# Splitting the first context load, its product and their order at the start of a cross-attention kernel

## The chip, the cores and the metric

The kernel runs on one core of a Trainium2 chip. The metric is the device time of one execution in microseconds (us); the median of three runs of the kernel before is 794.72 us (794.46 to 795.08). A core has five engines that work side by side and wait for one another through semaphores: TensorE (PE in the profile, with its weight loads as PEld), VectorE (DVE), ScalarE (ACT), GpSimd (POOL) and SyncE (SP), which here issues nearly all transfers (DMAs). Each engine takes its instructions strictly in the order of the program.

## What is computed

The inputs are `x` (8 x 128 x 512) and a context (8 x 128 x 512), all float32. The reference, cut to what matters:

```python
x = x + xattn(layernorm(x), ctx, ctx, mask, Wq, Wk, Wv, Wo)   # 32 query heads, 8 key/value heads of 128
x = x + ffn(layernorm(x), nf4(w1), nf4(w2), nf4(w3))          # weights quantized to NF4 and back, H = 1376
# in xattn:  k = rope(ctx @ Wk);  v = ctx @ Wv;  q = rope(layernorm(x) @ Wq)
#            softmax over 30*tanh(q.k*scale/30), masked, times v, times Wo
```

Only `k = rope(ctx @ Wk)` is touched by the change, and of it only the first of the 16 key products.

## The kernel before, in words

**Precision by halves.** A float32 operand is split in two fp32r tiles, a high part and a low part. `split` (lines 154 to 156) does it: ScalarE casts the source into the high part (line 155), then VectorE or GpSimd subtracts that from the source into the low part (line 156). `product` (lines 165 to 171) makes a float32 product of three matmuls for each slice of the contraction: high weights with low data (line 169), high with high (line 170), low with high (line 171). The contraction is 512 long, in KT = 4 slices of 128, so one product is 12 matmuls.

**Stages.** The kernel first computes all keys and values and stores them to DRAM, then runs 64 attention steps, then the feed-forward part. The change lies in the first microseconds of the first stage. This stage works through a list written out by hand, `tiles` (line 571): `("k", kv, half)` is the key product of head `kv` over one half of the context's 1024 rows (512 of them), `("v", j, b)` a value product, `("q", 0, g)` a first query product. It begins k(0,0), k(1,0), k(2,0), k(0,1), k(1,1), k(2,1), then values and keys take turns.

**Key product.** `k_proj` (line 511) writes pk(kv, half), one PSUM bank of 128 x 512, from the split weights `wkt[kv]` and the split, transposed context `cT`. Banks with the tag "q" are two in number, so k(2,0) has to wait until k(0,0)'s bank has been read. The reading is `rope` (line 454): two ScalarE copies of half the partitions each, from PSUM into `rs_k` with the halves exchanged (lines 461, 462), a VectorE product of PSUM with the cosine table into `rc_k` (line 463), a GpSimd product of `rs_k` with the sine table (line 464), and an addition into `kr` (line 465; on VectorE for heads 0 to 2). `rs_k` and `rc_k` have two buffers each. The loop at line 628 sets the order: at tile n it emits the rope of tile n-1 without its addition, then the product n, then the addition of tile n-2, then what `advance(n)` gives, then the extras of `plan[n]`.

**Loads.** `loads` (line 585) lists what is loaded and the tile from which on its split may be emitted. `advance(n)` (line 592) issues loads ahead of time, as long as `early` (the eight accumulator tiles, not yet needed, used as landing buffers) has buffers or fewer than four loads wait for their split, and it emits the splits that are due, in list order. All loads go through SP's queue. Before, the order at the start is:

```python
loads = [(-1, "k", 0, 0)] + [(-1, "c", 0, k) for k in range(KT)]
loads += [(-1, "t", 0, 0), (-1, "k", 1, 0), (0, "k", 2, 0), (0, "c", 1, 0), (0, "c", 1, 1), (1, "c", 1, 2), (1, "c", 1, 3)]
```

Here ("k", kv) is the key weights of head kv, 256 KB; ("c", half, k) is slice k of the context's half `half`, 128 x 512 floats, 256 KB in rows of 2 KB; "t" is the table of cosines and sines `tab`, 2 x 128 x 128 floats, 128 KB in rows of 512 bytes. In the text they are called wk0, c00 to c03, the table, wk1, wk2, c10 to c13. The low part of wk0 and of the context is made on VectorE, that of wk1 and wk2 on GpSimd. The splits of wk2, c10 and c11 are emitted at tile 0, so ahead of the rope of k(0,0); those of c12 and c13 at tile 1, behind it.

Of the kernel before, what the change touches and what calls it, by code (L numbers as in the profile page):

```python
# [20 lines left out]
P = 128  # L21
# [4 lines left out]
KT = D // P  # L26
# [36 lines left out]
def block_kernel(ctx: ExitStack, tc: tile.TileContext, x, ctxt, mask, wq, wk, wv, wo, w1, w2, w3, w12t, w3_t,  # L63
                 rope_tab, nf_bias, out):
    nc = tc.nc
    V, S, Q, E = nc.vector, nc.scalar, nc.gpsimd, nc.tensor
# [9 lines left out]
    def bank(tag, name):  # L76
        shape = [P, 1024 if tag == "pv" else 512]
        return ps.tile(shape, F32, tag=tag, name=name, bufs=2 if tag == "q" else 1)[:, :512]
# [75 lines left out]
    def split(hi, lo, src, engine):  # L154
        S.copy(hi, src)
        engine.tensor_tensor(lo, src, hi, ALU.subtract)  # L156
# [5 lines left out]
            E.transpose(pt[:, k * P:(k + 1) * P], src[:, k * P:(k + 1) * P], ident)  # L162
        return lambda: split(hi, lo, pt.rearrange("p (k t) -> p k t", k=KT), V)

    def product(out, pairs, start=True, stop=True):

        n = len(pairs)
        for i, ((ah, al), (bh, bl)) in enumerate(pairs):
            E.matmul(out, ah, bl, start=start and i == 0, stop=False)  # L169
            E.matmul(out, ah, bh, start=False, stop=False)  # L170
            E.matmul(out, al, bh, start=False, stop=stop and i == n - 1)  # L171


    def scales(a, r, w):
# [251 lines left out]
    with ExitStack() as c1:  # L426
# [9 lines left out]
        early = list(acc)  # L436

        def stage(src, shape, name):
            if early:
                raw = early.pop(0)  # L440
            else:
                raw = raw_pool[-1].tile([P, 512], F32, tag="raw", name=f"raw_{name}", bufs=3 if len(raw_pool) > 1 else 4)
            if len(shape) == 3:
                raw = raw.rearrange("p (k n) -> p k n", k=shape[1])
            nc.sync.dma_start(raw, src)
            return raw
# [7 lines left out]
        def rope(dst, src, cos, sgn, name, engine=None):  # L454

            hd = HD // 2
            every = lambda ap: ap.unsqueeze(1).to_broadcast([P, 4, T])
            src4 = src.rearrange("p (b t) -> p b t", t=T)
            c = tp.tile([P, 4, T], F32, tag="t1", name=f"rc_{name}")
            s = tp.tile([P, 4, T], F32, tag="t2", name=f"rs_{name}")  # L460
            S.copy(s[:hd], src4[hd:])
            S.copy(s[hd:], src4[:hd])  # L462
            V.tensor_tensor(c, src4, every(cos), ALU.mult)  # L463
            Q.tensor_tensor(s, s, every(sgn), ALU.mult)  # L464
            return lambda: (engine or Q).tensor_tensor(dst, c, s, ALU.add)  # L465
# [6 lines left out]
        def q_proj(u, g):  # L472
            kv, half = divmod(u, 2)
            if g == 0:
                qr[u] = a1.tile([P, 4, G, T], F32, tag="qr", name=f"qr_{u}", bufs=2)
            pq = bank("q", f"pq_{u}_{g}")
            w, t = wqt[kv, g], xT[half]
            product(pq, [((w[:, 0, k], w[:, 1, k]), (t[:, 0, k], t[:, 1, k])) for k in range(KT)])
            return lambda: rope(qr[u][:, :, g, :], pq, cosq, sgnq, f"q{u}_{g}", V if u < 2 else None)


        with ExitStack() as c3:
# [4 lines left out]
            cT = [kv1.tile([P, KT, B * T], F32R, name=f"cT_{i}", bufs=1) for i in range(2)]  # L487
# [3 lines left out]
            def load_c(half, k):  # L491
                cols = slice(half * 512, half * 512 + 512)
                raw = stage(ctxt[k * P:(k + 1) * P, cols], [P, 512], f"c_{half}_{k}")
                return lambda: split(cT[0][:, k, cols], cT[1][:, k, cols], raw, V)

            def load_v(j, k):
                raw = stage(wv[k * P:(k + 1) * P, j * 512:(j + 1) * 512], [P, 512], f"wv_{j}_{k}")
                if (j, k // 2) not in wvt:
                    wvt[j, k // 2] = kv1.tile([P, 2, 2, 512], F32R, tag="wv", name=f"wv_{j}_{k}", bufs=3)
                t = wvt[j, k // 2]  # L500
                return lambda: split(t[:, 0, k % 2], t[:, 1, k % 2], raw, (V, Q)[j])
# [9 lines left out]
            def k_proj(kv, half):  # L511
                cols = slice(half * 512, half * 512 + 512)
                pk = bank("q", f"pk_{kv}_{half}")
                w = wkt[kv]
                product(pk, [((w[:, 0, k], w[:, 1, k]), (cT[0][:, k, cols], cT[1][:, k, cols])) for k in range(KT)])

                def later():
                    kr = kv1.tile([P, 512], F32, tag="kr", name=f"kr_{kv}_{half}")
                    add = rope(kr.rearrange("p (b t) -> p b t", t=T), pk, tab[:, 0], tab[:, 1], f"k{kv}_{half}",
                               V if kv < 3 else Q)  # L520

                    def last():
                        add()
                        nc.sync.dma_start(kr_d[kv, half], kr)
                    return last
                return later

            def v_proj(j, b):
                own = slice(b * T, b * T + T)
                pv = bank(("pv", "wo")[b % 2], f"pvp_{j}_{b}")  # L530
                product(pv, [((cT[0][:, k, own], cT[1][:, k, own]),
                              (wvt[j, k // 2][:, 0, k % 2], wvt[j, k // 2][:, 1, k % 2])) for k in range(KT)])

                def later():
                    v = vs[:, b % 4]
                    S.copy(v, pv.rearrange("p (a d) -> p a d", a=4))
                    return lambda: nc.sync.dma_start(
                        v_d[4 * j:4 * j + 4, :, b, :].rearrange("a p d -> p a d"), v)
                return later
# [26 lines left out]
            def normal(b):  # L566
# [8 lines left out]
                     ("v", 1, 1), ("k", 7, 1)] + [("v", 1, b) for b in range(2, B)] + [("q", 0, g) for g in range(G)]  # L575
            make = {"k": k_proj, "v": v_proj, "q": q_proj}
            plan = [[] for _ in range(len(tiles) + 1)]


            def load_tab(*_):  # L580
                nc.sync.dma_start(tab, rope_tab.rearrange("c d t -> d c t"))
                return lambda: None

            load = {"t": load_tab, "k": load_k, "c": load_c, "v": load_v, "q": load_first_q}
            loads = [(-1, "k", 0, 0)] + [(-1, "c", 0, k) for k in range(KT)]
            loads += [(-1, "t", 0, 0), (-1, "k", 1, 0), (0, "k", 2, 0), (0, "c", 1, 0), (0, "c", 1, 1), (1, "c", 1, 2), (1, "c", 1, 3)]
            loads += [(2, "v", 0, 0), (2, "v", 0, 1), (3, "v", 0, 2), (3, "v", 0, 3), (5, "k", 3, 0), (9, "k", 4, 0)]
            loads += [(12, "k", 5, 0), (15, "k", 6, 0), (17, "v", 1, 0), (18, "v", 1, 1), (19, "k", 7, 0)]
            loads += [(20, "v", 1, 2), (21, "v", 1, 3)] + [(24 + 2 * g, "q", g, 0) for g in range(G)]
# [78 lines left out]
        def where(i):  # L668
            u, bb = divmod(i, 4)
            return u, u // 2, (u % 2) * 4 + bb, bb  # L670
# [88 lines left out]
        for i in range(N):  # L759
            u, kv, b, bb = where(i)  # L760
# [101 lines left out]
    pairs = {}  # L862
    for b, i in down:
# [5 lines left out]
        for h in range(4 * i, min(NHT, 4 * i + 4)):  # L869
            m = min(P, H - h * P)  # L870
            t, s = w3t[h].rearrange("p i k c -> p i (k c)"), hs[b, i]
# [7 lines left out]
        elif i == 2:  # L879
            o = f1.tile([P, D], F32, tag="o", name=f"o_{b}", bufs=4)  # L880
            parts = 2 if b == B - 1 else 1
            for j in range(parts):
                own = slice(j * D // parts, (j + 1) * D // parts)
# [38 lines left out]
```

## Time and profile before

| what | value |
|---|---|
| median of 3 runs | 794.72 us |
| the profiled execution's own time | 795.47 us |
| its span, first to last instruction | 793.7 us |
| mean granted TensorE clock | 0.998 |
| busy: PE, PEld | 779.9 us (98%), 628.8 us (79%) |
| busy: DVE, ACT, POOL | 633.7 us (80%), 586.3 us (74%), 469.4 us (59%) |
| PE busy, 5 to 10 us | 3.11 of 5.00 us |
| PE busy, 20 to 100 us | 79.55 of 80.00 us |

Busy times are sums over an engine's instructions in one profiled execution; the span is that of the same execution, and 1.77 us of the execution's time lie around the span. A matmul's end is modelled and overlaps the next one, so the pace of matmuls is read from start to start: 0.23 us apart for 512 columns. In the timeline each row gives the start, the length, the engine, the line, the operation, the tiles out<-in, and in square brackets how long the engine had been idle and what ended that. "SPq" is SP issuing a transfer: its length is the time of the issue, not of the transfer.

### The profile page before, as it was taken

To read this page: it belongs to the slowest core of one execution; us is meant where nothing else is said; L and a number is where in the kernel's file an instruction comes from. 1 tells how busy PE (TensorE), PEld (TensorE's weight loads), DVE (VectorE), ACT (ScalarE), POOL (GpSimd) and SP (SyncE) were. 2 spreads that over 40 slices of the span, in tenths; PEclk is the share of its full clock that TensorE was granted. 3 is DMA by queue.
4 is the path that set the end of the run, shared out by engine and by line. 5 is a ranking of instruction groups with operands and counts; after the bars stand their busy time and mean duration, and the time that the engine had idled before them with its cause. 6 is when DMAs were issued, how large, how long until landed. Compare 5 with 4: busy or idle time off the path is not lost.

```text
span 793.7 us, 11197 instructions
## 1 busy us (share of the span) xinstructions
PE 779.9 (98%) x3737; PEld 628.8 (79%) x3737; DVE 633.7 (80%) x840; ACT 586.3 (74%) x821; POOL 469.4 (59%) x411
## 2 busy tenths in 40 slices
PE   7999998999999999999999999999999999999998
PEld 5788876878787877878787787878778888888877
DVE  5757679888888887888888878888877688889971
ACT  6448668889796978888797879898732588779740
POOL 3569546588787877876887877788642223232100
PEclk9999999999999999999999999999999999999999
DMA  6966735537236444627253533341313162651011
GB/s 220 299 180 212 212 104 165 158 83 211 69 113 176 138 120 121 173 81 224 76 172 109 139 83 134 108 159 28 107 54 107 54 182 84 185 160 55 3 61 46
DMA packets 73457, 102.44 MB, mean 129 GB/s; under 512 B 7832, under 2 KB 42968, under 8 KB 73400
## 3 DMA queue, kind: packets, MB, share of 16 engines
q1 hardware_dynamic: 70232, 90.19, 38.0%
q0 software_dynamic: 3168, 11.54, 4.7%
q8 instruction: 30, 0.49, 0.3%
q14 instruction: 27, 0.22, 0.1%
HBM read 79.32 MB, written 22.38 MB: 128 GB/s over the span
## 4 chain that ended last, share of the span: by engine, by line
PE 89%; ACT 4%; DVE 3%; issue 1%; POOL 1%; DMA 1%; SPq 0%; DVEq 0%; ACTq 0%; POOLq 0%
PE pq L169 7%; PE pq L171 7%; PE pq L170 7%; PE po L171 7%; PE pl L675 7%; PE pv L688 6%; PE po L170 6%; PE po L169 6%; PE pt_a L162 3%; PE pd L169 3%; PE pd L170 3%; PE pd L171 3%; PE pu L171 3%; PE pg L171 3%; PE pg L170 3%; PE pu L170 3%
## 5 line engine op out<-in xcount | busy, mean ns | idle before, releaser
L201 DVE SCALAR_TENSOR_TENSOR nc_w<-nm_w,nc_w 128x1024 f32<-128x1024 bf16 (+1 forms) x238 | 284.6, 1196 | 57.6 <-ACT nm_w L195 47.2
L195 ACT ACTIVATE nm_w<-w_w,bias 128x1024 bf16<-128x1024 f32 (+1 forms) x255 | 276.0, 1116 | 19.8 <-POOL w_w L205 9.4
L681 POOL TENSOR_TENSOR th<-th,mt 128x512 f32<-128x512 f32 x64 | 84.3, 1317 | 81.4 <-ACT th L679 64.7
L169 PE MATMUL pq<-xT,wq 128*128 128x512 f32 x256 | 124.7, 487 | 0.0
L171 PE MATMUL po<-wo,aT 128*128 128x512 f32 x256 | 100.4, 392 | 1.1 <-DVE aT L156 1.1
L169 PE MATMUL po<-wo,aT 128*128 128x512 f32 x256 | 101.4, 396 | 0.1
L171 PE MATMUL pq<-xT,wq 128*128 128x512 f32 x256 | 100.4, 392 | 0.0
L170 PE MATMUL pq<-xT,wq 128*128 128x512 f32 x256 | 100.1, 391 | 0.0
L170 PE MATMUL po<-wo,aT 128*128 128x512 f32 x256 | 100.0, 391 | 0.0
L464 POOL TENSOR_TENSOR rs_q<-rs_q,sgnq 128x512 f32<-128x512 f32 x64 | 83.2, 1299 | 14.4 <-ACT rs_q L462 14.4
L678 ACT ACTIVATE th<-pl 128x512 f32<-128x512 f32 x64 | 38.3, 598 | 52.9 <-PE pl L675 50.4
L465 POOL TENSOR_TENSOR qr<-rc_q,rs_q 128x512 f32<-128x512 f32 x56 | 72.7, 1298 | 0.0
L688 PE MATMUL pv<-vt,th 128*128 128x129 f32 x512 | 68.5, 277 | 2.5 <-POOL th L681 2.4
L675 PE MATMUL pl<-qr,krt 128*128 128x512 f32 x128 | 67.1, 607 | 0.0
L169 PEld LDWEIGHTS pq<-xT,wq 128*128 128x128 f32 x256 | 48.3, 189 | 22.8 <-issue 11.2
L170 PEld LDWEIGHTS pq<-xT,wq 128*128 128x128 f32 x256 | 48.4, 189 | 22.6 <-issue 14.2
L688 PEld LDWEIGHTS pv<-vt,th 128*128 128x128 f32 x512 | 62.7, 193 | 3.1 <-POOL th L681 3.1
L205 POOL TENSOR_TENSOR w_w<-w_w,s_w 128x1024 f32<-128x1024 f32 (+1 forms) x17 | 39.5, 2326 | 35.3 <-DMA s_w<-scale_d 31.6
L463 DVE TENSOR_TENSOR rc_q<-pq,cosq 128x512 f32<-128x512 f32 x64 | 44.0, 687 | 19.7 <-ACT rs_q L462 18.6
L171 PEld LDWEIGHTS po<-wo,aT 128*128 128x128 f32 x256 | 48.0, 188 | 12.2 <-DVE aT L156 2.0
L169 PEld LDWEIGHTS po<-wo,aT 128*128 128x128 f32 x256 | 48.1, 188 | 12.0 <-issue 1.6
L171 PEld LDWEIGHTS pq<-xT,wq 128*128 128x128 f32 x256 | 48.1, 188 | 10.9
(145 smaller groups left out, 1696.0 us busy)
## 6 DMA issues: line engine op xcount, KB each, us to landing
w12t_d<-dqt SPq DMA_DIRECT2D x22, 512.0 KB
w<-w12t_d POOLq DMA_DIRECT2D x22, 512.0 KB, 4.5
s_w<-scale_d SPq DMA_DIRECT2D x40, 256.0 KB
raw_wq<-in_L_xattn_Wq SPq DMA_DIRECT2D x32, 256.0 KB
raw_wo<-in_L_xattn_Wo SPq DMA_DIRECT2D x32, 256.0 KB
s_w<-scale_d SPq DMA_DIRECT2D x86, 64.0 KB
ws<-in_L_ffn_w SPq DMA_DIRECT2D x20, 256.0 KB
w_w<-in_w12t SPq DMA_DIRECT2D x10, 512.0 KB
```

The lines of the kernel that those rows point to most:

```text
L169: E.matmul(out, ah, bl, start=start and i == 0, stop=False)
L170: E.matmul(out, ah, bh, start=False, stop=False)
L171: E.matmul(out, al, bh, start=False, stop=stop and i == n - 1)
L195: S.activation(m, self.w, AF.Relu, bias=bias[:self.p, i:i + 1], scale=BIG if up else -BIG)
L201: V.scalar_tensor_tensor(self.c, m, step, self.c, ALU.min, ALU.subtract if i == POS[0] else ALU.add)
L205: Q.tensor_tensor(self.w, self.w, self.s, ALU.mult)
L463: V.tensor_tensor(c, src4, every(cos), ALU.mult)
L464: Q.tensor_tensor(s, s, every(sgn), ALU.mult)
L465: return lambda: (engine or Q).tensor_tensor(dst, c, s, ALU.add)
L675: E.matmul(pl, krt[kv, u % 2][:, bb * T:(bb + 1) * T], qr[u][:, bb].rearrange("p g t -> p (g t)"), start=True, stop=True)
L681: Q.tensor_tensor(em[i], em[i], mt.unsqueeze(1).to_broadcast([P, G, T]), ALU.mult)
L688: E.matmul(pv[:, g, :HD + 1], em[i][:, g], vt[kv][:, b], start=True, stop=True)
```

## The change

The first half of the context is loaded in two rounds of four transfers: columns 0 to 255 of all four slices, then columns 256 to 511, each 128 KB in rows of 1 KB, into the two halves of the same four landing buffers. Each piece is split by itself. The product k(0,0) is made as two products of 256 columns, one over each round, into the two halves of the same bank. In these two products the order within a slice is high-high, low-high, high-low. The table's load and its place in the list move behind wk1. All other products keep their order. Nothing else in the kernel differs.

```diff
-    def product(out, pairs, start=True, stop=True):
+    def product(out, pairs, start=True, stop=True, high=False):
...
         for i, ((ah, al), (bh, bl)) in enumerate(pairs):
-            E.matmul(out, ah, bl, start=start and i == 0, stop=False)
-            E.matmul(out, ah, bh, start=False, stop=False)
-            E.matmul(out, al, bh, start=False, stop=stop and i == n - 1)
+            three = [(ah, bh), (al, bh), (ah, bl)] if high else [(ah, bl), (ah, bh), (al, bh)]
+            for j, (a, b) in enumerate(three):
+                E.matmul(out, a, b, start=start and i + j == 0, stop=stop and i == n - 1 and j == 2)
...
+            def load_first_c(part, k):
+                cols = slice(part * 256, part * 256 + 256)
+                if part == 0:
+                    first[k] = early.pop(0)
+                raw = first[k][:, cols]
+                nc.sync.dma_start(raw, ctxt[k * P:(k + 1) * P, cols])
+                return lambda: split(cT[0][:, k, cols], cT[1][:, k, cols], raw, V)
...
-                product(pk, [((w[:, 0, k], w[:, 1, k]), (cT[0][:, k, cols], cT[1][:, k, cols])) for k in range(KT)])
+                parts = 2 if (kv, half) == (0, 0) else 1
+                for j in range(parts):
+                    own = slice(j * 512 // parts, (j + 1) * 512 // parts)
+                    product(pk[:, own], [((w[:, 0, k], w[:, 1, k]), (cT[0][:, k, cols][:, own], cT[1][:, k, cols][:, own]))
+                                         for k in range(KT)], high=parts == 2)
...
-            loads = [(-1, "k", 0, 0)] + [(-1, "c", 0, k) for k in range(KT)]
-            loads += [(-1, "t", 0, 0), (-1, "k", 1, 0), (0, "k", 2, 0), (0, "c", 1, 0), (0, "c", 1, 1), (1, "c", 1, 2), (1, "c", 1, 3)]
+            loads = [(-1, "k", 0, 0)] + [(-1, "f", part, k) for part in range(2) for k in range(KT)]
+            loads += [(-1, "k", 1, 0), (-1, "t", 0, 0), (0, "k", 2, 0), (0, "c", 1, 0), (0, "c", 1, 1), (1, "c", 1, 2), (1, "c", 1, 3)]
```

The eight pieces are called f00 to f03 (first round) and f10 to f13 (second round) in the text.

More of the change, by code (lines that the diff above doesn't have):

```diff
@@ L494, in load_c @@
                 return lambda: split(cT[0][:, k, cols], cT[1][:, k, cols], raw, V)
+            first = {}
+            def load_first_c(part, k):
[5 more added lines that the diff above has]
+                return lambda: split(cT[0][:, k, cols], cT[1][:, k, cols], raw, V)
             def load_v(j, k):
@@ L582, in load_tab @@
                 return lambda: None
-            load = {"t": load_tab, "k": load_k, "c": load_c, "v": load_v, "q": load_first_q}
-            loads = [(-1, "k", 0, 0)] + [(-1, "c", 0, k) for k in range(KT)]
-            loads += [(-1, "t", 0, 0), (-1, "k", 1, 0), (0, "k", 2, 0), (0, "c", 1, 0), (0, "c", 1, 1), (1, "c", 1, 2), (1, "c", 1, 3)]
+            load = {"t": load_tab, "k": load_k, "c": load_c, "f": load_first_c, "v": load_v, "q": load_first_q}
+            loads = [(-1, "k", 0, 0)] + [(-1, "f", part, k) for part in range(2) for k in range(KT)]
+            loads += [(-1, "k", 1, 0), (-1, "t", 0, 0), (0, "k", 2, 0), (0, "c", 1, 0), (0, "c", 1, 1), (1, "c", 1, 2), (1, "c", 1, 3)]
             loads += [(2, "v", 0, 0), (2, "v", 0, 1), (3, "v", 0, 2), (3, "v", 0, 3), (5, "k", 3, 0), (9, "k", 4, 0)]
```

## The prediction

> **What bounds the kernel now.** I read the page first: PE is busy for 779.9 of 793.7 us, so only a stretch where PE waits can give anything. The change touches only the first 12 us. I therefore read the chain that ended last, cut at 32 us:
>
> ```profile
> 4.53 6.26 DMA acc<-in_ctx
> ...
> 10.81 0.63 ACT cT L155
> ...
> 11.47 0.04 DVE cT L156
> ...
> 13.75 0.25 DVE rc_k L463
> ...
> 16.64 1.20 DVE kr L465
> ...
> 17.92 0.59 ACT rs_k L461
> ...
> 22.32 0.70 DVE rc_k L463
> 23.07 0.50 PE pk L169
> ```
>
> The reader is to see that the chain does not go through k(0,0). It starts at the landing of c10 (10.79 us), the transfer *behind* everything that the change splits, goes through the splits of the second half and the ropes, and reaches PE only at 23.07 us, where k(2,1) waits for the bank of k(0,1). From there on it is matmul after matmul, and PE is busy for 79.55 of the 80 us from 20 to 100 us, so a shift at 23.07 us reaches the end in full.
>
> Next, the timeline of ACT, POOL, DVE and PE between 9 and 15 us:
>
> ```profile
> 9.42 1.29 ACT L155 CAST wk<-acc 128x512 fp32r<-128x512 f32 x2 [0.46 <-DMA acc<-in_L_xattn_Wk]
> 10.12 2.56 POOL L156 TENSOR_TENSOR wk<-acc,wk 128x512 fp32r<-128x512 f32 x2 [8.80 <-DMA acc<-in_L_xattn_Wk]
> 11.47 0.50 PE L171 MATMUL pk<-cT,wk 128*128 128x512 f32 x1 [0.29 <-POOL wk L156]
> 11.47 1.76 DVE L156 TENSOR_TENSOR cT<-acc,cT 128x512 fp32r<-128x512 f32 x1 [1.78 <-ACT cT L155]
> 14.49 0.50 PE L169 MATMUL pk<-cT,wk 128*128 128x512 f32 x1 [0.46 <-DVE rc_k L463]
> ```
>
> Here k(1,0) waits for the low part of wk1 (11.47), and k(2,0) waits for the rope of k(0,0) (14.49). The subtraction of c10 takes 1.76 us against 0.69 us for the same shape earlier: it begins in the middle of POOL's work on wk1 and wk2 and ends 0.55 us after that work (12.68), so it stood nearly still.
>
> Last, what carries the loads: SP's issues, the DMA share (last two columns: share, GB/s) in two half-microseconds, and packet counts of 5.9 to 7.5 us and of 9 to 10 us:
>
> ```profile
> 5.01 1.15 SPq L445 DMA_DIRECT2D raw_c<-in_ctx  x1
> ```
> ```profile
> 4.00:4.50 0.50, 0.50 (x4) 0.50 (x3) 0.24 (x1) 0.48 (x2) 0.00 (x0) 1.00 0.57 184
> 7.50:8.00 0.50, 0.50 (x3) 0.27 (x2) 0.00 (x0) 0.50 (x1) 0.00 (x0) 1.00 1.09 400
> ```
> ```profile
> DMA packets 446, 0.55 MB, mean 345 GB/s; under 512 B 37, under 2 KB 223, under 8 KB 446
> ```
> ```profile
> DMA packets 184, 0.34 MB, mean 338 GB/s; under 512 B 19, under 2 KB 19, under 8 KB 184
> ```
>
> From 6 us on the DMA engines are full; the transfers are bound by bytes, with a hole around 4.5 us.
>
> **The loads.** Issues are 0.47 us apart (1.19, 1.65, 2.12). Four more put 4 x 0.47 = 1.9 us ahead of all that follows: wk1's issue moves from 3.54 to about 4.95, wk2's to 5.9, c10's from 4.53 to 6.4 us. What hides this is the queue in the DMA engines. A load with nothing ahead of it, wk0, took 2.9 us from its issue (0.75) to its cast (3.61). At that price c10 could land at 9.3, wk2 at 8.8, wk1 at 7.9 us, and bytes let them land at about 10.8, 10.1 and 9.1; so the cover is 1.2 us at the least, and what is missing of it is paid in full. SP also holds back: the 12th load was issued at 7.46, when the 4th landed, the 13th at 8.34, when the 5th landed. After, c10 is the 13th and its partner is f03, which lands near 5.9 us, ahead of 6.4: no wait. c11 to c13 are issued up to 1 us later; ACT took c12 only at 13.31, and the stream was empty after 12.5 us.
>
> The Trainium skill speaks against this part: "DMA: Bandwidth & Descriptors", section "Anatomy of one DMA", prices a transfer at some 2.0 us plus its bytes at 436 GB/s (measured on the GpSimd path), and its section on bandwidth asks for 1 MiB at a time. As the fixed part of four more transfers in a row that is 8 us, an estimate. The trace has c02, c03 and wk1 land 0.9 to 1.1 us apart with 256 KB each: the fixed part of one lies beside the bytes of another. I take the trace: nothing for the four, as long as the cover holds.
>
> Rows of 1 KB are not in this stretch. From both sides: in 9 to 10 us the 165 packets of 2 KB take 16 us of engine time, 97 ns each. In 5.9 to 7.5 us, 25.2 us of engine time less 223 x 97 ns leave 3.6 us for 186 packets of the table's 512 bytes, 19 ns each. So cost goes by bytes, or a little below: 1024 packets of 1 KB for 512 of 2 KB cost nothing. If each were priced like a 2 KB packet, it would be 1024 x 48 ns / 16 = 3.1 us. I take 0.1 us, by the nearer row, for the eight completions and unevenness.
>
> **The table** moves 128 KB out of wk1's way: at 350 GB/s 0.37 us, so wk1 lands at about 9.1 (9.42 less 0.37, plus the 0.1). wk2 and c10 have the same bytes ahead as before: 10.9 for c10. The table itself is not read before 13.36 us.
>
> **The splits.** No row has 128x256 in a cast; between 128x384 (513 ns) and 128x512 (620 ns) the slope gives 0.40 us. VectorE's 128x256 row is 421 ns (line 886). So ACT has 8 x 0.40 less 4 x 0.62 = 0.7 us more, DVE 8 x 0.42 less 4 x 0.69 = 0.6 us more. From 5 to 10 us ACT is busy for 2.44 and DVE for 2.66 of 5 us: it fits into waits for transfers. Without that cover it would come on wk1's cast. The last piece, f13, with c03's landing at 8.34 has its cast done at 8.75 and its subtraction at 9.2, against 9.68.
>
> **The product.** 24 matmuls of 256 columns at 0.12 us (start to start in the last output) are 2.88, before 12 x 0.23 = 2.72: 0.16 us more, in PE's idle time. With high parts first only the last matmul waits for the subtraction of f13: k(0,0) ends near 9.4 instead of 10.55 us, 1.1 us sooner. This is the visible gain, and almost all of it is lost at once: k(0,0)'s rope began only at 12.11, 1.5 us after its product, because ACT first casts wk2, c10 and c11. So k(0,0) is not late now, and being earlier moves only the wait.
>
> **What does move.** wk1's cast ends at 9.75, its low part on POOL at 11.1 instead of 11.4, and k(1,0) runs on 0.3 us sooner. POOL's second one ends at 12.4 instead of 12.68, and with it the held subtraction of c10 at 12.9 to 13.0. But ACT's order, bound to c10, is 0.1 us later: copies of k(0,0) end at 13.4, of k(1,0) at 15.75. POOL's rs_k of k(1,0) cannot start before these and held the addition of k(0,0) until 17.84. Before, it began at 15.72 and took 1.56 us instead of 1.3, so 0.3 us is to be had there at most. The step to 17.92 gains between 0.35 (VectorE's side alone) and minus 0.1 (ACT's side alone); I take 0.15, between them, as both alternate on the path. From 17.92 the ropes pace themselves (17.92, 21.12, 24.29, 3.2 us each) down to 23.07.
>
> **Sum.** 23.07 becomes 22.9; the span 793.7 - 0.15 = 793.55, the profiled execution's 795.47 becomes 795.3 (1.8 us lie around the span). The median of the runs is 0.75 us below that execution: 794.72 - 0.15 = 794.6 us.
>
> **Rivals.** A measurement of this kernel can tell about 0.2% (1.6 us) from no change.
> - *The loads run better (0.19).* Between 4 and 5.5 us 260 KB move where the full rate makes 570: 0.8 us lost. If smaller pieces fill the hole, c10 and wk2 land 0.8 us sooner, and with the table's share the chain is 0.9 us earlier: 793.8. For it: ACT and DVE follow c10 directly. Against it: six loads were issued and not landed at 4.5 us, and the engines still paused. With everything at its best (1.6 us or more, 0.04 of the 0.19) it is faster by over 0.2%.
> - *The issue becomes the bound (0.17).* c11's issue took 1.15 instead of 0.43 us: SP was held with seven loads out. Twice the rows for the same bytes could hold wk2 and c10 the same way, up to 0.7 us each, beyond the cover by half: 0.6 us later, 795.3.
> - *Slower: short rows (0.09).* In the queue ahead of wk1, 1 KB packets cost as much as 2 KB ones: 3.1 us on every load behind, thus c10 near 13.9 and the chain 3.0 us late: 797.7. It passes 1.6 us from about 74 ns a packet on. Against it: the 512-byte packets at 19 ns. A fall of the clock would end here too; but PE was granted 1.00 from 5 to 10 us at 3.11 busy of 5, and the longest new gap is some 1.5 us.
> - *Likeliest (0.55):* the gain of the first product is spent in waits, minus 0.5 to plus 0.4 us: 794.6.
>
> **The numbers.** The range 793.5 to 795.8 takes in the likeliest case, most of the first rival and the second; left out are the short rows and the far ends. Faster by over 0.2%: 0.04; slower: 0.09; within: 0.87.
>
> **What would show it.** k(0,0)'s last matmul near 9.4 us, then PE idle until wk1's low part near 11.1; c10's cast near 10.9; the copies of k(0,0) still behind c11's cast at about 12.2; k(2,1)'s start near 22.9. I am wrong if c10's cast comes before 10.2 or after 11.5, if PE's first wait after 9.4 ends elsewhere, or if the shift at k(2,1) is not the shift at the end.

## The result, and the profile after

The change made the kernel slower. The median of 11 runs is 796.62 us (796.05 to 798.43), beside 794.95 us (794.46 to 795.55) in 11 runs of the kernel before on the same chip: a ratio of 1.0024, 95% interval 1.0016 to 1.0031. The forecast was 794.6 us, its range ended at 795.8.

One caution for all that follows: a profile shows a single execution. That of before (795.47 us) lies near the top of its kernel's spread, that of after (796.05 us, span 794.3) is the lowest of its eleven. So the two profiles stand only 0.6 us apart where the medians stand 1.67 us apart, and a row of one profile carries a conclusion below only where several kernels repeat it.

First the chain that ended last, of after, cut at 32 us (start, length, what):

```profile
5.53 0.38 SPq L597
...
6.47 0.43 SPq L446
...
6.94 5.04 DMA raw_c<-in_ctx
...
12.01 0.62 ACT cT L155
...
12.65 0.58 ACT rs_k L462
...
13.85 0.63 ACT cT L155
...
16.85 1.28 DVE kr L466
...
18.21 0.58 ACT rs_k L462
...
22.62 0.70 DVE rc_k L464
...
23.37 3.04 PE pk L172 x12
```

The path ends as before, but its first part differs. Before, it entered through c10, whose cast began at 10.81 us with c11's cast directly behind it, and it went on through VectorE's subtractions. Now it enters through c11, one load later, and goes on through ScalarE: c11's cast, the copies of k(0,0), the casts of c12 and c13. SP's issues stand in the chain itself: c10 is issued at 6.47 us instead of 4.53, c11 at 6.94 instead of 5.01. From c11's cast to k(2,1) it is 11.36 us now (12.01 to 23.37), and was 11.61 before (11.46 to 23.07).

Then the timeline of PE and ACT in after:

```profile
8.88 0.84 PE L172 MATMUL pk<-cT,wk 128*128 128x256 f32 x3 [0.20 <-ACT cT L155]
11.25 2.56 PE L172 MATMUL pk<-cT,wk 128*128 128x512 f32 x10 [0.63 <-POOL wk L156]
14.60 8.57 PE L172 MATMUL pk<-cT,wk 128*128 128x512 f32 x36 [0.80 <-DVE rc_k L464]
8.42 0.41 ACT L155 CAST cT<-acc 128x256 fp32r<-128x256 f32 x1 [0.65 <-DMA acc<-in_ctx]
10.26 0.62 ACT L155 CAST wk<-acc 128x512 fp32r<-128x512 f32 x1 [0.43 <-DMA acc<-in_L_xattn_Wk]
10.96 0.62 ACT L155 CAST cT<-acc 128x512 fp32r<-128x512 f32 x1
12.01 0.62 ACT L155 CAST cT<-raw_c 128x512 fp32r<-128x512 f32 x1 [0.42 <-DMA raw_c<-in_ctx]
12.65 0.58 ACT L462 COPY rs_k<-pk 64x512 f32<-64x512 f32 x1
```

k(0,0)'s last three matmuls begin at 8.88 us and end at 9.72, so the product ends 1.0 us sooner than before (10.72). Its rope's first copy begins at 12.65 us, 0.54 later than before (12.11): ScalarE reaches it only behind c11, for which it stood idle. PE's wait for wk1's low part ends at 11.25 us, its wait for k(0,0)'s rope at 14.60, behind the same two as before.

Last, the busy time in the stretches 5.5 to 6 and 9 to 11 us (last two columns: share of the DMA engines, GB/s), first before, then after:

```profile
5.50:6.00 0.50, 0.36 (x2) 0.32 (x3) 0.09 (x1) 0.12 (x1) 0.00 (x0) 1.00 0.87 262
9.00:11.00 2.00, 2.00 (x8) 1.21 (x8) 0.69 (x1) 1.43 (x3) 0.88 (x1) 1.00 1.03 371
```
```profile
5.50:6.00 0.50, 0.28 (x2) 0.00 (x1) 0.02 (x1) 0.46 (x2) 0.00 (x0) 1.00 0.57 172
9.00:11.00 2.00, 1.46 (x5) 0.66 (x5) 0.28 (x1) 1.27 (x3) 1.09 (x1) 1.00 0.94 308
```

Before, the DMA engines are full while wk2 and c10 land. After, they move 308 GB/s instead of 371 there, and from 5.5 to 6 us 172 instead of 262, nearly half empty. So the stream has gaps now where it was bound by bytes. The fourteen profiles (before, after and the twelve runs below) repeat this: from 5 to 11 us the engines moved 320 to 345 GB/s in the seven with at most eight loads issued ahead of c10, and 253 to 296 in the seven with more. The granted clock (the column ahead of these two) is 1.00 in both.

### The profile page after: what moved, and what is told of

It reads as the page before. It is cut to its first block, busy times and chain, and to the rows that moved or that the text cites. A ratio compares the mean times of both kernels' runs of the same rounds, so it can differ in the third digit from the quotient of the medians.

```text
span 794.3 us, 11237 instructions
## 1 busy us (share of the span) xinstructions
PE 780.9 (98%) x3749; PEld 630.4 (79%) x3749; DVE 632.1 (80%) x844; ACT 586.6 (74%) x825; POOL 468.0 (59%) x411
## 4 chain that ended last, share of the span: by engine, by line
PE 83%; DVE 5%; ACT 5%; issue 3%; DMA 2%; POOL 1%; SPq 1%; POOLq 0%; DVEq 0%; ACTq 0%
PE po L172 19%; PE pq L172 19%; PE pg L172 8%; PE pu L172 8%; PE pl L691 6%; PE pv L704 6%; PE pvp L172 6%; PE pk L172 4%; PE pd L172 3%; PE pt_a L162 3%; ACT nm_w L196 2%; DVE nc_w L202 1%; DMA raw_c<-in_ctx 1%; DVE xn_y L150 1%; DMA krt<-kr_d 1%
## 5 line engine op out<-in xcount | busy, mean ns | idle before, releaser
L172 PE MATMUL pq<-xT,wq 128*128 128x512 f32 x768 | 210.9, 424 | 0.0
L172 PE MATMUL po<-wo,aT 128*128 128x512 f32 x768 | 188.0, 393 | 1.1 <-DVE aT L156 1.0
L172 PEld LDWEIGHTS po<-wo,aT 128*128 128x128 f32 x768 | 143.8, 188 | 34.8 <-issue 2.3
L172 PE MATMUL pg<-xT,w 128*128 128x512 f32 x264 | 63.7, 390 | 0.0
L172 PE MATMUL pu<-xT,w 128*128 128x512 f32 x264 | 63.5, 389 | 0.0
L172 PE MATMUL pd<-w3t,hs 128*128 128x512 f32 (+3 forms) x297 | 61.1, 366 | 0.9 <-DVE o L902 0.9
L172 PEld LDWEIGHTS pd<-w3t,hs 128*128 128x128 f32 (+1 forms) x297 | 51.3, 189 | 10.8 <-issue 1.3
L172 PEld LDWEIGHTS pu<-xT,w 128*128 128x128 f32 x264 | 49.6, 188 | 10.3
L172 PEld LDWEIGHTS pg<-xT,w 128*128 128x128 f32 x264 | 49.3, 188 | 10.1
L156 POOL TENSOR_TENSOR w3t<-w_w,w3t 128x512 fp32r<-128x512 f32 (+1 forms) x11 | 17.2, 1562 | 66.5 <-ACT w3t L155 66.5
```

The lines of the kernel that those rows point to most:

```text
L172: E.matmul(out, a, b, start=start and i + j == 0, stop=stop and i == n - 1 and j == 2)
```

## The experiments

Four theories were put to the test. **A, issues:** the loads behind the split ones come later because more transfers are issued ahead of them; in A1 their number counts, in A2 it is the rows of 1 KB. **B:** the time is lost later, at the start of the attention steps. **C, clock:** PE's gaps cost it a slower pace. **The product:** the new order or the halves of k(0,0) cost something. All of the twelve kernels in one table; "ahead" is the number of loads issued ahead of c10, the times are from each kernel's one profile, the ratio is that of the medians to the runs of before on the same chip:

| kernel | ahead | c10 issued | c10 cast | c11 cast | k(2,1) starts | median us | ratio (95%) |
|---|---|---|---|---|---|---|---|
| before | 8 | 4.53 | 10.81 | 11.46 | 23.07 | 794.95 | |
| after | 12 | 6.47 | 10.96 | 12.01 | 23.37 | 796.62 | 1.0024 (1.0016 to 1.0031) |
| e1: after, again | 12 | 6.44 | 11.39 | 12.04 | 23.39 | 796.87 | 1.0026 (1.0015 to 1.0036) |
| e2: before, table behind wk1 | 8 | 4.53 | 10.69 | 11.34 | 22.69 | 794.87 | 1.0002 (0.9993 to 1.0010) |
| e3: after with whole loads | 8 | 4.53 | 10.20 | 10.94 | 22.29 | 795.57 | 1.0010 (1.0004 to 1.0017) |
| e4: after with a whole product | 12 | 6.43 | 12.02 | 12.65 | 24.01 | 796.74 | 1.0026 (1.0016 to 1.0036) |
| e5: after, two slices a transfer | 8 | 4.68 | 10.69 | 11.50 | 22.83 | 795.17 | 0.9997 (0.9988 to 1.0005) |
| e6: after, second round on ScalarE | 12 | 6.45 | 12.04 | 12.65 | 24.02 | 796.80 | 1.0019 (1.0013 to 1.0026) |
| e7: before, four 8 KB transfers more | 12 | 6.43 | 12.07 | 12.73 | 24.09 | 796.82 | 1.0019 (1.0012 to 1.0025) |
| e8: after, PE kept busy | 12 | 6.43 | 11.33 | 12.41 | 23.78 | 796.70 | 1.0018 (1.0011 to 1.0025) |
| e9: before, first half in two transfers | 6 | 3.96 | 10.36 | 11.14 | 24.19 | 795.73 | 1.0011 (1.0004 to 1.0017) |
| e10: before, eight 8 KB transfers more | 16 | 8.33 | 13.22 | 13.88 | 25.22 | 798.27 | 1.0045 (1.0032 to 1.0059) |
| e11: e3, PE kept busy | 8 | 4.54 | 11.32 | 11.98 | 23.49 | 795.87 | 1.0010 (1.0004 to 1.0017) |
| e12: before, table behind c11 | 7 | 4.02 | 10.26 | 11.17 | 22.52 | 795.33 | 0.9999 (0.9991 to 1.0007) |

The median of before was 794.74 us beside e1 to e4, 795.33 beside e5 to e8, 795.15 beside e9 to e12; hence the ratios and not the medians are compared across the groups. Where a row differs from "after", "before" means the code before.

**e1, the changed kernel again.** No edit.

> The changed kernel once more, for a second execution's trace and for the spread of its times. Theory A (the start): the four additional issues put the landing of c11 late, and what an execution loses is lost before k(2,1) starts; then the start of k(2,1) is later than 23.07 us by about as much as the span is longer than 793.7 us (a span of 794.3 goes with 23.4 to 23.7, one of 796 with 25.4). Theory B (a later stage): k(2,1) starts at 23.3 to 23.5 us whatever the span, and the rest is lost at the start of attention near 118 us, where the changed kernel's chain went through a load of the keys. Theory C (the clock): the granted clock between 5 and 20 us is below 1.00. Time by all three: 796.6 us, plus or minus 0.5.

Measured: 796.87 us, 1.0026. The loss repeats. The span less the start of k(2,1) is 770.7 us (after 770.9, before 770.6), and over all fourteen profiles it lies between 770.5 and 771.1. So the stretch behind k(2,1) differs by 0.6 us at most, too little for the loss, and theory B falls: the greater part is made in the first 24 us.

**e2, only the table moved.**

```diff
# against before
-            loads += [(-1, "t", 0, 0), (-1, "k", 1, 0), ...
+            loads += [(-1, "k", 1, 0), (-1, "t", 0, 0), ...
```

> Only the table's load moved behind wk1; loads, splits and product as before. Theory A: no additional issue, so no loss: wk1's cast at about 9.1 us, c10's and c11's as before (10.8 and 11.5), 794.8 us plus or minus 0.4. Theory B: any shift of the start may upset the later stage: up to 796.5 us. Theory C: PE's idle time is unchanged: 794.9 us.

Measured: 794.87 us, 1.0002. wk1's cast begins at 8.44 us, c11's at 11.34 and k(2,1) at 22.69. Here too the path goes through ScalarE, and k(2,1) follows c11's cast by 11.35 us. It does so by 11.33 to 11.37 us in eleven of the fourteen profiles; the others are before's own (11.61), e9 and e11. The table's place neither costs nor gains anything that can be measured.

**e3, after with the four whole loads**; the product stays in two halves, high parts first.

```diff
# against after
-            loads = [(-1, "k", 0, 0)] + [(-1, "f", part, k) for part in range(2) for k in range(KT)]
+            loads = [(-1, "k", 0, 0)] + [(-1, "c", 0, k) for k in range(KT)]
```

> The changed kernel with the four whole slices of 512 columns loaded and split as before; the product in two halves with high parts first and the table's place are kept. The first half of the product now waits for the same four landings as the second. Theory A: the loss goes with the four issues: c10's cast near 10.8, c11's near 11.5, k(2,1) at 23.07 or a little earlier, 794.8 us plus or minus 0.4, although k(0,0) ends later than in the changed kernel. Theory C: PE idles longer before 9 us than in the changed kernel, so it is at least as slow: 796.6 us or more.

Measured: 795.57 us, 1.0010, with a wide spread (794.40 to 797.53). About 0.8 us of loss (0.3 to 1.4 by the interval) stays where the loads are whole. The profile doesn't show it: it caught an execution at the low end of that spread (span 792.8), with k(2,1) at 22.29.

**e4, after with the product of before**: the loads are split, the product is one of 512 columns in the old order.

```diff
# against after
-                parts = 2 if (kv, half) == (0, 0) else 1
+                parts = 1
```

> The changed kernel with k(0,0) as one product of 512 columns in the old order; the loads and splits in eight pieces and the table's place are kept. Theory A: as slow as the changed kernel, 796.6 us plus or minus 0.5, c11's cast near 12.0 us, though k(0,0) ends later. If the form of the product were the cause, 794.9 us.

Measured: 796.74 us, 1.0026, the whole loss. The split of the loads alone is enough to make it, and the new product gives nothing of it back. In the timelines of PE, ACT and SP of e4:

```profile
7.00 7.38 PE L172 MATMUL pk<-cT,wk 128*128 128x512 f32 x24 [1.96 <-DVE cT L156]
10.95 0.62 ACT L155 CAST wk<-acc 128x512 fp32r<-128x512 f32 x1 [1.10 <-DMA acc<-in_L_xattn_Wk]
12.02 0.62 ACT L155 CAST cT<-acc 128x512 fp32r<-128x512 f32 x1 [0.46 <-DMA acc<-in_ctx]
6.43 0.43 SPq L446 DMA_DIRECT2D acc<-in_ctx  x1
```

k(0,0) begins only at 7.00 us here, where after began it at 4.69, and yet the time is that of after. ScalarE's idle time ahead of wk2 and c10 ends with their landings, c10's 5.6 us behind its issue.

**e5, the same halves with half as many transfers**: one transfer brings 256 columns of two slices, still in rows of 1 KB. The splits and the product are those of after.

```diff
# against after
-                nc.sync.dma_start(raw, ctxt[k * P:(k + 1) * P, cols])
+                raw = early.pop(0).rearrange("p (k n) -> p k n", k=2)
+                nc.sync.dma_start(raw, ctxt[m * 2 * P:(m + 1) * 2 * P, cols].rearrange("(k p) n -> p k n", p=P))
```

> The changed kernel with the eight pieces loaded by four transfers: two slices of 256 columns each, 256 KB in rows of 1 KB. Same rows, as many issues as before the change. Theory A1 (each additional issue takes SP 0.47 us and what lies behind is issued later): c10 is issued at 4.5 us again, cast near 10.7; 794.9 us plus or minus 0.4. Theory A2 (rows of 1 KB load slower): as slow as the changed kernel, 796.6 us.

Measured: 795.17 us, 0.9997: the loss is gone. In the timelines of SP and ACT of e5:

```profile
1.19 1.96 SPq L501 DMA_DIRECT2D acc<-in_ctx  x4
4.68 0.43 SPq L446 DMA_DIRECT2D acc<-in_ctx  x1
11.50 0.62 ACT L155 CAST cT<-raw_c 128x512 fp32r<-128x512 f32 x1 [0.18 <-DMA raw_c<-in_ctx]
```

Four issues instead of eight, c10 issued at 4.68 us, c11's cast at 11.50: the place of before. The rows of 1 KB and the splits in halves are the same as in after, so A2 falls as the cause of the loss, and with it any price of the smaller splits that can be measured.

**e6, the second round issued by ScalarE** instead of SP.

```diff
# against after
-                nc.sync.dma_start(raw, ctxt[k * P:(k + 1) * P, cols])
+                (nc.scalar if part else nc.sync).dma_start(raw, ctxt[k * P:(k + 1) * P, cols])
```

> The changed kernel with the four pieces of the second round issued by ScalarE instead of SP; rows, pieces, splits and product as in the changed kernel. A1: SP issues c10 at 4.5 us again, its cast comes near 10.8; ScalarE pays four issues before its first cast, about 2.0 to 3.8 us, in its idle time; 794.9 us plus or minus 0.5. A2: 796.6 us.

Measured: 796.80 us, 1.0019: nothing gained. In the timelines of ACT and SP, and SP's waits (line, what it waited for, us in total, times, longest), of e6:

```profile
0.74 1.85 ACTq L505 DMA_DIRECT2D acc<-in_ctx  x4
1.19 1.36 SPq L505 DMA_DIRECT2D acc<-in_ctx  x3
3.92 0.62 ACT L155 CAST wk<-acc 128x512 fp32r<-128x512 f32 x1
4.03 0.33 SPq L505 DMA_DIRECT2D acc<-in_ctx  x1
6.45 0.43 SPq L446 DMA_DIRECT2D acc<-in_ctx  x1
```
```profile
SPq L505 <- DMA acc<-in_ctx: 1.5, 1, 1.5
SPq L597 <- DMA acc<-in_ctx: 0.6, 1, 0.6
```

The two engines did issue side by side, 0.46 us an issue on each. With wk0, three pieces from SP and four from ScalarE, eight loads were out at 2.6 us, and SP's fourth piece was then held to 4.03 us, until a context piece had landed. It was not enough that one load fewer was out: wk0 had landed by 3.92, when its cast began. In the trace the loads signal their landing on eight semaphores in turn, and what SP waited for was the landing of the load eight places back (ScalarE's first piece, 4.01 us). The table was held once more in that way (5.48). The 2.1 us of these waits stand where the saved 1.9 us of issues had been, and c10 is issued at 6.45 us, as in after. The Trainium skill ("DMA: Bandwidth & Descriptors", section "Rules for kernel authors") says that spreading transfers over issuing engines only saves issue time, not bandwidth. The rows agree on the issue; here even the saved time went, into the wait for a landing.

**e7, before with four transfers more that hardly move anything**: behind each slice of the first half 8 KB into a tile that nobody needs then.

```diff
# against before
+                if half == 0:
+                    nc.sync.dma_start(sgnq[:, k * 16:(k + 1) * 16], nf_bias)
```

> The kernel before with four additional transfers of 8 KB each, one behind each of c00 to c03, into a tile that is not yet in use: the additional issues of the change without its small rows, its splits or its product. A1: c10 is issued at 6.4 us and cast at 11.0 to 12.0; as slow as the changed kernel, 796.6 us plus or minus 0.5. A2: 794.9 us plus or minus 0.3, the 32 KB being too little to count.

Measured: 796.82 us, 1.0019. In the timelines of SP and ACT of e7, and its DMA row for 6 to 11 us:

```profile
6.43 0.43 SPq L445 DMA_DIRECT2D acc<-in_ctx  x1
12.07 0.62 ACT L155 CAST cT<-acc 128x512 fp32r<-128x512 f32 x1 [0.78 <-DMA acc<-in_ctx]
12.73 0.63 ACT L155 CAST cT<-raw_c 128x512 fp32r<-128x512 f32 x1
```
```profile
6.00:11.00 5.00, 4.21 (x14) 2.09 (x13) 2.08 (x3) 2.48 (x5) 0.86 (x1) 1.00 0.83 249
```

Loads, splits and product are those of before; only four small transfers are added, and the loss of the change is there, with c10's and c11's casts within 0.1 us of those in e4. Four transfers of 8 KB cost as much as the four more pieces of 128 KB. And the engines, which stood at a share of 1.03 from 6 to 11 us in before, now stand at 0.83.

**e8, after with PE kept busy**: two transposes that nobody reads behind each slice of the first product.

```diff
# against after
+            if high:
+                for _ in range(2):
+                    E.transpose(warm[:, :P], ident, ident)
```

> The changed kernel with two transposes of the identity into an unused bank after each slice of k(0,0), 16 in all, to keep PE busy while it waits for landings. Theory C (PE falls to half its clock in part of the executions because the 256-column matmuls leave it idle): back to 795.0 us with a narrower spread. Theory A: no change against the changed kernel, 796.6 us plus or minus 0.5, with the same spread of some 1.5 us.

Measured: 796.70 us, 1.0018. The loss stays, while PE is busy for all of 4.7 to 10 us. In after's own rows PE isn't slow either: its ten matmuls from 11.25 us on are 0.24 us apart on the mean. So theory C falls as the cause of the loss at the median.

**e9, fewer issues than before**: the first half as two transfers of 512 KB, two slices each.

```diff
# against before
-            loads = [(-1, "k", 0, 0)] + [(-1, "c", 0, k) for k in range(KT)]
+            loads = [(-1, "k", 0, 0)] + [(-1, "d", m, 0) for m in range(2)]
```

> The kernel before with the first context half loaded by two transfers of 512 KB (two slices each, rows of 2 KB, into a tile that is not yet in use) instead of four of 256 KB: two issues fewer. If issues bind only beyond the number of the kernel before, c10 is issued at about 3.6 us and nothing is won: 0 plus or minus 0.4 us against before. If each issue is worth its 0.47 us throughout, 0.9 us faster. The splits of c00 come later in either case, which nobody waits for in the end.

Measured: 795.73 us, 1.0011: slower, not faster. c10 is issued at 3.96 us and cast at 10.36, so the loads behind came somewhat earlier than in e2 (10.69). But in the timelines of PE and ACT of e9:

```profile
7.43 0.80 PE L169 MATMUL pk<-cT,wk 128*128 128x512 f32 x1 [2.39 <-DVE cT L156]
12.29 0.63 PE L171 MATMUL pk<-cT,wk 128*128 128x512 f32 x1
11.14 0.62 ACT L155 CAST cT<-raw_c 128x512 fp32r<-128x512 f32 x1 [0.16 <-DMA raw_c<-in_ctx]
12.96 0.59 ACT L461 COPY rs_k<-pk 64x512 f32<-64x512 f32 x1 [1.20 <-PE pk L171]
15.85 0.59 ACT L461 COPY rs_k<-pk 64x512 f32<-64x512 f32 x1 [0.55 <-PE pk L171]
```

The first slices land so late that k(0,0) begins at 7.43 us, and in this execution ScalarE's copies wait for PE: k(2,1) follows c11's cast by 13.05 us instead of 11.35. But two things came together. The product's matmuls are 0.43 us apart here, up to its last at 12.29; at 0.23 us apart it would have ended near 10.4 us (an estimate from these rows), before ScalarE had cast c11 at 11.76. And the profiled execution took 796.99 us, near the top of its kernel's spread (795.40 to 797.12). So the row shows what slow matmuls behind late slices can cost, 1.7 us; what makes up the 0.6 us of the median is not shown.

**e10, before with eight such small transfers**, two behind each slice.

```diff
# against before
+                if half == 0:
+                    for j in range(2):
+                        nc.sync.dma_start(sgnq[:, (2 * k + j) * 16:(2 * k + j + 1) * 16], nf_bias)
```

> The kernel before with eight additional transfers of 8 KB, two behind each of c00 to c03. Theory A1: a dose twice that of the four small ones, now beyond any cover, so 4 x 0.47 = 1.9 us more than those: 3.4 us slower than before, c10 issued at 8.3 us and cast at 13 to 14. If only the first few count, about 1.5 us slower as with four.

Measured: 798.27 us, 1.0045 (1.0032 to 1.0059), about twice e7's loss. In the timelines of SP and ACT of e10:

```profile
8.33 0.43 SPq L445 DMA_DIRECT2D acc<-in_ctx  x1
13.22 0.62 ACT L155 CAST cT<-acc 128x512 fp32r<-128x512 f32 x1 [1.04 <-DMA acc<-in_ctx]
```

Four issues more put c10 another 1.9 us back (6.43 to 8.33) and its cast 1.15 us. By the medians, four issues cost 1.5 us and eight 3.1 us: about 0.4 us each, close to the 0.47 us between two issues. e10 has only five runs, but its interval lies clear of e7's.

**e11, e3 with the transposes of e8**, to see whether e3's remaining 0.8 us come from PE.

> Whole loads and the product in halves, as in the run of that name that was 0.8 us slower than before with a wide spread, and two transposes of the identity after each slice of k(0,0) to keep PE busy. If those 0.8 us come from PE's clock falling to half while the narrow matmuls wait: back to 0 plus or minus 0.3 us against before, narrow. If they come from the order or form of the product itself: 0.8 us slower again.

Measured: 795.87 us, 1.0010: as slow as e3. In the timeline of ACT of e11:

```profile
11.98 0.62 ACT L155 CAST cT<-raw_c 128x512 fp32r<-128x512 f32 x1
15.15 0.59 ACT L465 COPY rs_k<-pk 64x512 f32<-64x512 f32 x1 [0.18 <-PE pk L172]
```

The transposes made PE late enough that a copy of k(1,0) had to wait for it, but only 0.18 us. This execution took 795.89 us, as the median, and the greater part of its loss lies in the landings: c11's cast begins 0.6 us later than in e2 and e5 (11.42 on the mean), with as many loads ahead. So the remaining loss is not shown to be PE's.

**e12, before with the table behind c11**, one issue fewer ahead of c10.

```diff
# against before
-            loads += [(-1, "t", 0, 0), (-1, "k", 1, 0), (0, "k", 2, 0), (0, "c", 1, 0), (0, "c", 1, 1), ...
+            loads += [(-1, "k", 1, 0), (0, "k", 2, 0), (0, "c", 1, 0), (0, "c", 1, 1), (0, "t", 0, 0), ...
```

> The kernel before with the table's load moved further back, behind c11: one issue and 128 KB fewer ahead of wk1, wk2, c10 and c11, nothing else changed. A candidate to beat both kernels: c10's and c11's casts 0.3 to 0.5 us earlier, the table still landing ahead of its first reader near 13 us, so 0.4 us faster than before, plus or minus 0.4. If the table comes later than that reader, slower by the difference.

Measured: 795.33 us, 0.9999. c10 is issued 0.5 us earlier than in before, and nothing is gained that can be measured. The interval, 0.7 us faster to 0.6 slower, leaves room for the 0.4 us that was expected, so the run doesn't show that an issue fewer than eight is worth nothing. No kernel of the twelve beats the kernel before.

## Why the prediction was wrong, point by point

**The step that failed** is in "The loads": "What hides this is the queue in the DMA engines", and "so the cover is 1.2 us at the least, and what is missing of it is paid in full." The 1.9 us of issues were counted rightly (c10's issue at 6.47 us, foretold 6.4). The cover was not there. I had priced the way from issue to landing at 2.9 us, by wk0, a load with nothing ahead of it. With others on the way c10 takes much longer. From issue to cast it took 6.3 us in before, 6.2 in e2, 5.7 in e3, 6.0 in e5, 6.8 in e11 and 6.2 in e12, with seven or eight loads ahead (mean 6.2); with twelve ahead 4.5 in after, 4.9 in e1 and e8, and 5.6 in e4, e6 and e7 (mean 5.2); with sixteen 4.9 in e10. A shorter way thus gave back some 1.0 of the 1.9 us on the mean, and the other 0.9 us was paid at c10. Put into my sum, an issue at 6.4 us and a way of 5.2 make 11.6 us, 0.8 later than the 10.8 that I had by the bytes: no cover at all.

A second entry of the same part was too small. I had c11 "issued up to 1 us later" and priced that at nothing. Its issue began 1.9 us later (5.01 to 6.94) and ended 1.2 later, and ScalarE turns to k(0,0)'s copies only behind c11's cast. In after, where c10's cast came as foretold (10.96 for 10.9), this is where the profile shows the loss: 12.01 instead of 11.46.

**The term that was mis-sized** is "nothing for the four". Measured are 1.7 us between the medians (1.3 to 2.5 by the interval of the ratio), 1.5 us with four transfers of 8 KB (e7), 3.1 with eight (e10). The rival "The issue becomes the bound", given 0.17 and 0.6 us, pointed at SP, but to a hold by the short rows that didn't come: in after wk2, c10 and c11 took 0.43 to 0.47 us to issue, and e5 has the short rows without the loss. To follow the sum in rows, I take the profiles of kernels whose profiled execution lay near their median. c11's cast begins at 11.34 and 11.50 us in e2 and e5 (mean 11.42) and at 12.65, 12.73 and 12.41 in e4, e7 and e8 (mean 12.60): 1.2 us later. k(2,1) begins at 22.69 and 22.83 against 24.01, 24.09 and 23.78, also 1.2 us later. The stretch behind k(2,1) is 0.4 us longer on the mean in these three profiles (771.0) than in those two (770.6), within its scatter over all fourteen. Together that is the 1.6 us between their spans; by the medians of the three kernels the loss is 1.4 to 2.0 us.

**The baseline.** I reasoned from one profile, and it was a late one. In e2, whose loads up to c03 are those of before, k(2,1) begins at 22.69 us, 0.4 earlier than in the profile that I started from. Its distance from c11's cast to k(2,1), 11.61 us, is also its own: the 0.15 us that I took as the change's gain behind c10 are not the change's, for e2 has the 11.35 us of after too. A slip that nothing hangs on: 12 x 0.23 us is 2.76, not 2.72.

**What held.**
- The path doesn't go through k(0,0): its last matmul began at 9.34 us (foretold 9.4), its copies still behind c11's cast, and e4 with the product of before has the same time. The gain of the first product, 1.0 us (foretold 1.1), was spent in waits, as foretold.
- wk1's low part released k(1,0) at 11.25 us (foretold 11.1), against 11.47 before.
- Casts of 256 columns took 0.41 us and the subtraction 0.42, as priced, and cost nothing that can be measured (e5).
- Rows of 1 KB cost nothing that can be measured (e5: 1.0 us faster to 0.4 slower by the interval), so the "short rows" rival with its 3.1 us falls. The slower side, given 0.09, came about by another way.
- The moved table costs nothing that can be measured (e2, e12).
- The shift at k(2,1) is the shift at the end to within 0.6 us: 770.5 to 771.1 us remain in all fourteen profiles.
- The rule that I weighed, a fixed price for every transfer, was set aside too lightly. Four transfers don't cost 8 us, but they don't cost nothing either: about 0.4 us each.

The tests that I had set would have told it only in part: c10's cast at 10.96 us in after is inside my bounds of 10.2 and 11.5, while c11's, of which I had said only that the copies would follow it at 12.2, is where the loss shows. In e4, e6 and e7 c10 itself is beyond the bound. That it came as foretold in after was luck of that execution: in the six profiles with twelve loads ahead its cast begins at 10.96 to 12.07 us.

**What stays open.** Why about 0.8 us remain in e3, where all loads are whole and only the product is made in halves: its one profile caught an execution at the low end of its spread, and e11 points at the landings without a reason for them. It doesn't show in e5, which has the same product. That the number of transfers makes the loss is shown (e5, e7, e10). Whether it does so by SP's time alone, or each transfer pays elsewhere as well, is not: in e6, the run that was to part the two, the hold took the saved time. What on a load's way takes the 4.5 to 5.6 us, with the DMA engines at a share of 0.83 in e7 and so not full, is not settled either: a longer way for each load and a slower service of several at once would look the same in these rows. Not tried: issuing wk1, wk2 and c10 ahead of the second round, which would keep the early first product without putting its issues ahead of c10.

## What to carry to other kernels

Count the issues ahead of the load that your path waits for, as you count its bytes: here each transfer beyond the eight ahead of it cost about 0.4 us, whether it moved 8 KB or 128 KB, and splitting a load to start its consumer sooner lost time because a more urgent one was queued behind. Price the way from issue to landing from a load in the same crowd (4.5 to 6.8 us here), never from the first one that has the queue to itself (2.9 us). And before you start an operation earlier, look at what its reader does until then: here ScalarE was busy with the casts of later loads or waited for them, and a product that ended 1.0 us sooner gained nothing.

## What the runs showed of the hardware that was not expected

- SP's next load was held in e6 for 1.5 us, until the load eight places back in the order of issue had landed (4.01 us), though that one was ScalarE's, the landing buffer was free, and wk0 had landed before it. In before the 12th and 13th loads went out in the same way, at the landings of the 4th and 5th (7.46 and 8.34 us). A second issuing engine brings forward only what this leaves room for.
- TensorE can run at half pace under a granted clock that reads 1.00. In e9 the matmuls of 512 columns follow each other 0.43 us apart from 8.03 to 12.72 us and 0.23 us apart after 13.13; e2 and e12 have such a stretch too, up to 9.76 and 10.65 us, at no cost that shows (k(2,1) follows c11's cast by 11.35 us in both). The row for 8 to 12 us:

```profile
8.00:12.00 4.00, 4.00 (x11) 3.10 (x10) 2.29 (x3) 2.93 (x6) 2.60 (x2) 1.00 0.92 313
```

The column ahead of the last two, the clock, says 1.00, and 11 matmuls fill 4 us. So the pace is read from start to start. What sets off such a stretch, no run here shows.
- The granted clock can halve without a cost where PE isn't on the path: in e4's profile it read 0.50 from 9 to 10 us, and k(2,1) follows c11's cast by 11.36 us, as in after, where it read 1.00.
